# Query and key projections of layer 1 by seven block products in place of eight

## The chip, the cores and the metric

The kernel runs on one core of a Trainium2 chip. The metric is the device time of one execution in microseconds (us). The kernel before takes 2162.17 us as the median of 3 runs (2159.51 to 2166.93).

## The reference, cut to what matters

128 graphs of 64 nodes with 256 features pass through four layers, each as `x = x + layer(relu(layernorm(x)))`, all in float32. Layer 0 mixes over the graph and runs four small LSTMs over windows of the nodes. Layer 1 is a graph convolution, then attention with 4 heads of 64, then a two-layer MLP:

```python
h = relu(layernorm(einsum('mn,bnf->bmf', L_norm, x) @ Wc + bc))
x1 = h + x
q, k, v = x1 @ Wq, x1 @ Wk, x1 @ Wv            # split into 4 heads
o = softmax(mask(q @ k.T / sqrt(64))) @ v      # per graph and head
x2 = layernorm(x1 + o @ Wo + bo)
out = layernorm(x2 + gelu(x2 @ W1 + b1) @ W2 + b2)
```

Layer 2 is a second attention, layer 3 a spectral step with the eigenvectors of a Laplacian. The change is in `q` and `k`: the product of a 256x256 weight with the transposed tokens.

## The kernel before, in words

Tokens are handled in tiles of 128 (two graphs); there are 64 tiles. Layer 0 takes them in 8 groups of 8 tiles, the later layers ("the rest", layers 1 to 3) in 16 groups of 4 tiles, which is 512 tokens. Layer 0 writes its result to memory ("put"), and a rest group fetches its 4 tiles from there. The eigenvectors are worked out on VectorE beside layer 0.

The order of the work is not the order in which it is written. Every operation is recorded (so all instructions have one line, L344) and a planner, `Plan.schedule`, lists them for each engine in turn. It knows a cost for each operation, the buffers of each pool and what each operation depends on, keeps several rest groups in flight (8 of them), ranks by group and by the length of the path still ahead, and adds 0.4 us of distance between a producer on another engine and a TensorE operation of the rest (`slack`). Each engine then executes its list in order: an instruction that waits holds up everything behind it on its engine. So any edit to the recorded operations can move others. Small 64x64 products are kept together in bursts of 32 or 16 (`plan.burst()`), and TensorE changes between bursts and other work as seldom as the planner can arrange.

The pools that matter: `bank`, the 8 PSUM banks of 128x512; `big`, buffers of 128x1024 in SBUF, to which the spaces called `arena`, `sums`, `mids` and parts of `Whh` are added once layer 0 is done with them; `stat`, small ones for the statistics of layer norms. Weights of layers 1 to 3 are loaded by SyncE's queue (SP) into the space of LSTM weights (`Wih`, `Whh`) as these become free near the end of layer 0; `Carver` deals that space out. That is why a layer 1 weight shows in the profile as `Wih` or `Whh`, and a `big` buffer often as `arena`, `sums` or `mids`.

In layer 1 (`layer1`), once `x1` is done, `to_fm` transposes it to `x1T` (2 chunks of 128 features by 512 tokens) by 8 transposes and 2 copies out of PSUM. `proj_fm` then makes half of `qT` or `kT` by two products of 128x512 that accumulate in one bank; `evac` copies the bank to SBUF, on VectorE if its last argument is even and on ScalarE if it is odd. So q and k take 8 products of 128x512 and 4 copies of 128x512, two of them on each engine. After the softmax `pT` (transposed attention) and `oT` (the attention's output) are each copied out by one copy on VectorE and one on ScalarE.

Layer 0 has the 7-product scheme already: `lstm_fast` splits weights and inputs into 2x2 blocks, `pieces` makes four sums of the input blocks, and `fastw` holds the sums of weight blocks. There, each of the seven products is a pair of matmuls (input and hidden part).

Of the kernel before, what the change touches and what calls it, by code (L numbers as in the profile page):

```python
# [8 lines left out]
ALU = mybir.AluOpType  # L9
# [878 lines left out]
P = 128  # L888
# [4 lines left out]
HT = 4  # L893
# [39 lines left out]
def gnn_kernel(ctx: ExitStack, tc: tile.TileContext, a, out):  # L933
# [4 lines left out]
    def C(shape, name):  # L938
        return pool.tile(list(shape), F32, name=name)
# [3 lines left out]
    wih = [C([P, 2 * (3 if p == 0 else 4) * D], f"Wih{p}") for p in range(4)]  # L943
    whh = [None] + [C([P, 8 * D], f"Whh{p}") for p in range(1, 4)]
# [36 lines left out]
    plan = Plan(tc, {"PE": nc.tensor, "V": nc.vector, "ACT": nc.scalar, "G": nc.gpsimd, "SP": nc.sync}, pools, late, reserve, window, EIG, REST + NT // HT - 6, slack)  # L981
    PE, V, ACT, G, SP = (plan.proxy(e) for e in ("PE", "V", "ACT", "G", "SP"))

    def bank(name):
        return plan.value("bank")

    def load(t, src):
        SP.dma_start(t, src)
        return t

    def chunks(src):
        return src.rearrange("(c p) f -> p c f", p=P)
# [25 lines left out]
    Wg = [load(C([P, 2, D], f"Wg{i}"), chunks(a[f"Wg{i}"])) for i in range(2)]  # L1018
# [59 lines left out]
    for p in (1, 2):  # L1078
        fastw[p] = []
        for i, w in enumerate((Wih[p], Whh[p])):  # L1080
            a11, a12, a21, a22 = (w.rearrange("p k (q m n) -> p k q m n", q=4, m=2)[:, k, :, m, :] for m in range(2) for k in range(2))
            s1, s2, s4 = (space.tile([P, 4, P]) for j in range(3))
            s3 = a21 if i else space.tile([P, 4, P])
# [21 lines left out]
    room = Carver(arena)  # L1105
# [53 lines left out]
    flat = lambda t: t.rearrange("p t f -> p (t f)")  # L1159
# [17 lines left out]
    def tm(n=HT, f=D):  # L1177

        return plan.value("big")[:, :n * f].rearrange("p (t f) -> p t f", f=f)

    def fm():

        return plan.value("big")[:, :2 * HT * P].rearrange("p (c n) -> p c n", c=2)
# [4 lines left out]
    def transposes(srcs):  # L1188

        pt = bank("tr")  # L1190
        for i, s in enumerate(srcs):
            PE.transpose(pt[:, i * P:(i + 1) * P], s, ident)
        return pt
# [51 lines left out]
    def pieces(B, eng):  # L1245

        n = B(0, 0).shape
        w = 1
        for k in n[1:]:
            w *= k  # L1250
        t = plan.value("big")[:, :4 * w].rearrange("p (i n) -> p i n", i=4)
        t = [t[:, i] for i in range(4)]
        if len(n) == 3:
            t = [v.rearrange("p (w t) -> p w t", t=n[2]) for v in t]
        eng.tensor_tensor(t[0], B(0, 1), B(0, 0), op=ALU.subtract)
        eng.tensor_tensor(t[1], B(1, 1), t[0], op=ALU.subtract)
        eng.tensor_tensor(t[2], B(1, 1), B(0, 1), op=ALU.subtract)
        eng.tensor_tensor(t[3], B(1, 0), t[1], op=ALU.subtract)
        return {1: B(0, 0), 2: B(1, 0), 3: B(1, 1), 4: t[3], 5: t[0], 6: t[1], 7: t[2]}
# [128 lines left out]


    plan.group = WEIGHTS  # L1390
    room = Carver(wih[1], whh[1], wih[2], whh[2], wih[0])
    wtile = lambda src: load(room.tile([P, src.shape[0] // P, src.shape[1]]), chunks(src))
    btile = lambda src, n=D: load(room.tile([P, n]), src.to_broadcast([P, n]))
    ctile = lambda shape, src: load(room.tile(shape), src)
    Wc, Wq, Wk, Wv, W1, W2, Wo = (wtile(a[n]) for n in ("Wc", "Wq", "Wk", "Wv", "W1", "W2", "Wo"))
# [2 lines left out]

    g2c, be2c = (ctile([P, 2], a[n].rearrange("o (c p) -> p (o c)", p=P)) for n in ("g2", "be2"))
    G.tensor_tensor(b2, b2, be2, op=ALU.add)  # L1400
    W2a = wtile(a["L2_W"])

    wa = room.tile([P, 2, D])
    WT, a12 = fm(), wtile(a["L2_a"])
# [25 lines left out]
    def evac(dst, src, i):  # L1430
        if i % 2:
            ACT.copy(dst, src)
        else:
            V.tensor_copy(dst, src)
# [8 lines left out]
    def proj_fm(w, src, m):  # L1443
        ps = bank("fm")
        for c in range(2):
            PE.matmul(ps, w[:, c, tok(m)], src[:, c, :], start=c == 0, stop=c == 1)
        return ps

    def proj_tm(lhs, w, nk, t0):

        ps = bank("tm")
        for t in range(2):
            for c in range(nk):
                PE.matmul(ps[:, t * D:(t + 1) * D], lhs(c, t0 + t), w[:, c, :], start=c == 0, stop=c == nk - 1)
        return ps
# [29 lines left out]
    def layer1(x):  # L1485
        h = relu_norm(x)
        lx = mix_fm(h, lambda t: lapb)
        x1 = tm()
        for t0 in (0, 2):
            ps = proj_tm(lambda c, t: lx[:, c, tok(t)], Wc, 2, t0)  # L1490
            V.tensor_add(x1[:, t0:t0 + 2, :], ps.rearrange("p (t f) -> p t f", t=2), vec(bc, 2))
        norm(x1)
        for t0 in (0, 2):
            xp, hp = x1[:, t0:t0 + 2, :], h[:, t0:t0 + 2, :]
            V.tensor_mul(xp, xp, vec(g1, 2))
            G.tensor_add(xp, xp, vec(be1, 2))
            V.scalar_tensor_tensor(xp, xp, 0.0, hp, op0=ALU.max, op1=ALU.add)
        x1T = to_fm(x1)
        qT, kT, v = fm(), fm(), tm()
        for m in range(2):  # L1500
            evac(qT[:, m, :], proj_fm(Wq, x1T, m), 0)
            evac(kT[:, m, :], proj_fm(Wk, x1T, m), 1)
        for t0 in (0, 2):
            evac(pair(v, t0), proj_tm(lambda c, t: x1T[:, c, tok(t)], Wv, 2, t0), 1)
        for t0 in (0, 2):
            G.tensor_add(x1[:, t0:t0 + 2, :], x1[:, t0:t0 + 2, :], vec(bo, 2))


        ps = [bank("qk") for m in range(2)]
        with plan.burst():  # L1510
            for b, m, r in [(b, m, r) for b in range(2 * HT) for m in range(2) for r in range(2)]:
                PE.matmul(ps[m][half(r ^ m), bat(b)], qT[half(r), m, bat(b)], kT[half(r), m, bat(b)], start=True, stop=True)
        s = tm(4 * HT, N)
        for m in range(2):
            sm = s[:, m * 2 * HT:(m + 1) * 2 * HT, :]
            V.scalar_tensor_tensor(sm, ps[m].rearrange("p (b k) -> p b k", k=N), 0.125, vec(mask1, 2 * HT), op0=ALU.mult, op1=ALU.add)
            stat = plan.value("stat")
            softmax_shift(sm, stat[:, :2 * HT])
            ACT.activation(sm, sm, AF.Exp)
            ssum = stat[:, 2 * HT:4 * HT]  # L1520
            V.reduce_sum(ssum, sm, axis=AX.X)
            V.reciprocal(ssum, ssum)
            G.tensor_mul(sm, sm, ssum.unsqueeze(2).to_broadcast([P, 2 * HT, N]))

        pT = fm()
        for m in range(2):
            evac(pT[:, m, :], transposes([flat(s[:, (m * HT + t) * 2:(m * HT + t) * 2 + 2, :]) for t in range(HT)]), m)
        oT = fm()

        po = [bank("o") for i in range(2)]  # L1530
        with plan.burst():
            for m, t, i, r in [(m, t, i, r) for m in range(2) for t in range(HT) for i in range(2) for r in range(2)]:
                PE.matmul(po[i][half(r), bat(m * HT + t)], v[half(i), t, bat(2 * m + r)], pT[half(i), m, bat(2 * t + (r ^ m))], start=True, stop=True)
        for i in range(2):
            evac(oT.rearrange("p c (t b n) -> p c t b n", t=HT, b=2)[:, :, :, i, :], po[i].rearrange("p (c t n) -> p c t n", c=2, t=HT), i)
        x2 = tm()
        for t0 in (0, 2):
            ps = proj_tm(lambda c, t: oT[:, c, tok(t)], Wo, 2, t0)
            V.tensor_add(x2[:, t0:t0 + 2, :], ps.rearrange("p (t f) -> p t f", t=2), x1[:, t0:t0 + 2, :])
        norm(x2)  # L1540
        x2T = fm()
        for c in range(2):
            ACT.activation(x2T[:, c, :], transposes([x2[:, t, tok(c)] for t in range(HT)]), AF.Identity, scale=g2c[:, c:c + 1], bias=be2c[:, c:c + 1])
        V.tensor_mul(x2, x2, vec(g2))
        for t0 in (0, 2):
            G.tensor_add(x2[:, t0:t0 + 2, :], x2[:, t0:t0 + 2, :], vec(b2, 2))
        mT = [fm() for i in range(2)]
        for m in range(4):
            ACT.activation(mT[m // 2][:, m % 2, :], proj_fm(W1, x2T, m), AF.Gelu, bias=b1[:, m:m + 1])
        for t0 in (0, 2):  # L1550
            ps = proj_tm(lambda c, t: mT[c // 2][:, c % 2, tok(t)], W2, 4, t0)
            V.tensor_add(pair(x2, t0), ps, pair(x2, t0))
        for t0 in (0, 2):
            G.tensor_add(x[:, t0:t0 + 2, :], x[:, t0:t0 + 2, :], vec(be3, 2))
        norm(x2)
        for t0 in (0, 2):
            V.tensor_mul(x2[:, t0:t0 + 2, :], x2[:, t0:t0 + 2, :], vec(g3, 2))
            V.tensor_add(x[:, t0:t0 + 2, :], x[:, t0:t0 + 2, :], x2[:, t0:t0 + 2, :])
# [115 lines left out]
```

## Time and profile before

| | |
|---|---|
| median of 3 runs | 2162.17 us |
| the profiled execution's own time | 2164.86 us |
| its span, first to last instruction | 2163.1 us |
| TensorE (PE) busy | 2117.6 us, 98% |
| VectorE (DVE) busy | 1795.0 us, 83% |
| ScalarE (ACT) busy | 1066.5 us, 49% |
| GpSimd (POOL) busy | 650.6 us, 30% |
| granted TensorE clock, mean | 0.993 |

The page gives busy time by engine, then the span in 40 slices with busy tenths, then the chain that ended last, then groups of instructions as `out<-in`, with count, busy time, mean duration of one, and the idle time of the engine just before them. A float32 matmul leaves two MATMUL records (16580 records in all). A record's end is modelled, so durations of successive matmuls overlap; the pace is read from the starts. Layer 0 ends at about 1367 us of the span; the rest groups, which begin to be mixed in at 1222 us, fill what follows.

### The profile page before, as it was taken

What the parts mean: (1) busy time and instruction counts of PE and PEld (TensorE: products, weight loads), DVE (VectorE), ACT (ScalarE), POOL (GpSimd) and SP (SyncE); (2) the same over time, 40 slices, a digit from 0 to 9 for tenths busy, and PEclk for the clock granted to TensorE, in tenths of its full rate; (3) what the DMA queues carried; (4) which work ended last, traced back from release to release, by engine and by line L of the source; (5) the groups of instructions that cost most, each with busy time, mean ns of one, the idle gap of its engine ahead of it and who ended that gap; (6) DMA issues with size and microseconds to landing.
All of it is one profiled execution on the core that took longest, in us unless ns stands there. A gap on an engine that the chain in (4) does not pass through costs nothing. (4 is left out here: it accounts for less than half of the span.)

```text
span 2163.1 us, 45587 instructions
## 1 busy us (share of the span) xinstructions
PE 2117.6 (98%) x16580; PEld 1632.8 (75%) x16580; DVE 1795.0 (83%) x7402; ACT 1066.5 (49%) x2321; POOL 650.6 (30%) x968
## 2 busy tenths in 40 slices
PE   9999999999999999999999999999999999999997
PEld 6688688688678688678778788767677777676776
DVE  5788888888899999889989887777887778875796
ACT  3354354354344344345345343555556656545673
POOL 7211221210200110110110101675456555644353
PEclk9999999999999999999999999999999999999999
DMA  5000100100100100100000111200010000000001
GB/s 205 1 3 22 41 3 21 40 1 21 40 1 20 40 1 20 40 1 20 26 1 21 52 44 44 89 1 21 1 41 21 22 21 21 11 21 2 1 2 60
DMA packets 44865, 57.66 MB, mean 27 GB/s; under 512 B 8928, under 2 KB 38496, under 8 KB 44640
## 3 DMA queue, kind: packets, MB, share of 16 engines
q1 hardware_dynamic: 43536, 53.71, 7.5%
q8 instruction: 130, 2.13, 0.4%
q10 hardware_dynamic: 1104, 1.05, 0.2%
q14 instruction: 95, 0.78, 0.1%
HBM read 37.53 MB, written 16.78 MB: 25 GB/s over the span
## 5 line engine op out<-in xcount | busy, mean ns | idle before, releaser
L344 PE MATMUL bank<-big,Wih 128*128 128x256 f32 (+3 forms) x2400 | 751.8, 436 | 14.4 <-DVE arena L344 6.7
L344 PEld LDWEIGHTS bank<-big,Wih 128*128 128x128 f32 x2400 | 440.3, 191 | 194.0 <-issue 112.1
L344 ACT ACTIVATE mids<-bank,bl 128x256 f32<-128x256 f32 (+3 forms) x528 | 274.6, 526 | 387.5 <-PE bank L344 385.3
L344 PE MATMUL bank<-big,Whh 128*128 128x256 f32 (+2 forms) x1624 | 431.5, 367 | 3.7 <-DVE big L344 3.7
L344 DVE TENSOR_TENSOR arena<-arena 64x21 f32<-64x21 f32 (+5 forms) x2251 | 372.1, 195 | 29.8 <-POOL arena L344 1.3
L344 PEld LDWEIGHTS bank<-big,Whh 128*128 128x128 f32 x1624 | 294.1, 190 | 42.8 <-issue 9.9
L344 PE MATMUL bank<-big,sums 128*128 128x168 f32 (+2 forms) x1664 | 267.5, 310 | 0.3
L344 POOL TENSOR_SCALAR stat<-stat 128x4 f32<-128x4 f32 (+1 forms) x228 | 71.1, 313 | 561.8 <-DVE stat L344 547.9
L344 PEld LDWEIGHTS bank<-big,sums 128*128 128x128 f32 (+1 forms) x1664 | 223.6, 179 | 17.2 <-issue 4.5
L344 ACT COPY mids<-bank 128x168 f32<-128x168 f32 (+2 forms) x378 | 124.8, 349 | 147.7 <-PE bank L344 142.9
L344 DVE TENSOR_TENSOR big<-mids 128x512 f32<-128x512 f32 (+2 forms) x256 | 141.8, 563 | 36.1 <-ACT mids L344 32.9
L344 ACT ACTIVATE mids<-mids,bl 128x336 f32<-128x336 f32 (+3 forms) x192 | 102.0, 539 | 77.6 <-DVE mids L344 73.6
L344 DVE SCALAR_TENSOR_TENSOR arena<-arena 64x1 f32<-64x1 f32 (+15 forms) x565 | 122.3, 239 | 6.2 <-POOL arena L344 2.5
L344 POOL TENSOR_TENSOR stat<-stat,mhalf 128x4 f32<-128x4 f32 (+1 forms) x114 | 121.9, 1070 | 6.4
L344 ACT ACTIVATE mids<-big 128x256 f32<-128x256 f32 (+2 forms) x176 | 89.4, 510 | 67.6 <-DVE big L344 48.0
L344 DVE TENSOR_TENSOR mids<-bank,mids 128x168 f32<-128x168 f32 (+1 forms) x294 | 103.1, 356 | 8.4 <-PE bank L344 4.7
L344 DVE TENSOR_SCALAR arena<-arena 64x1 f32<-64x1 f32 (+8 forms) x533 | 103.1, 200 | 8.4 <-POOL arena L344 0.4
L344 DVE TENSOR_TENSOR big<-big,mids 128x256 f32<-128x256 f32 (+2 forms) x192 | 93.7, 488 | 11.0 <-ACT mids L344 10.0
L344 POOL TENSOR_TENSOR big<-big 128x168 f32<-128x168 f32 (+1 forms) x24 | 15.8, 671 | 262.0 <-DVE arena L344 135.8
L344 POOL TENSOR_TENSOR arena<-arena 64x1 f32<-64x1 f32 x66 | 44.8, 678 | 152.6 <-ACT arena L344 106.3
L344 DVE BATCH_NORM_STATS2 stat<-big 128x6 f32<-128x256 f32 x228 | 83.2, 406 | 4.9 <-DMA big<-put 4.0
L344 ACT COPY big<-bank 128x512 f32<-128x512 f32 x90 | 49.5, 586 | 58.0 <-PE bank L344 55.9
(366 smaller groups left out, 3663.0 us busy)
## 6 DMA issues: line engine op xcount, KB each, us to landing
big<-in_x_dram SPq DMA_DIRECT2D x30, 512.0 KB, 5.3
put<-big SPq DMA_DIRECT2D x16, 512.0 KB, 2.8
arena<-put SPq DMA_DIRECT2D x8, 512.0 KB, 6.8
out_dram<-arena SPq DMA_DIRECT2D x16, 256.0 KB, 2.2
big<-put SPq DMA_DIRECT2D x7, 512.0 KB, 4.4
out_dram<-big SPq DMA_DIRECT2D x14, 256.0 KB, 2.4
Wih<-in_WihT_dram SPq DMA_DIRECT2D x3, 1024.0 KB, 12.1
Whh<-in_WhhT_dram SPq DMA_DIRECT2D x3, 1024.0 KB, 13.8
```

What stands on the lines that cost most here:

```text
L344: getattr(self.engines[op.eng], name)(*map(real, args), **{k: real(a) for k, a in kw.items()})
```

## The change

Four edits:

1. When weights are loaded, three new 128x128 tiles for each of Wq and Wk are made on GpSimd, by four operations per weight; the fourth result overwrites a block of the weight itself. The tiles come out of the same space as the other weights (768 columns), so some later tiles get other places, and the space of `Wg` is added at the end of the list.
2. Per rest group, `pieces` makes four 128x256 sums of blocks of `x1T` on GpSimd, in one more `big` buffer.
3. `proj_fast` replaces two `proj_fm` and two `evac` for q, and the same for k: seven products of 128x256 where there were four of 128x512. Two banks are held; results are read out of PSUM while the bank goes on accumulating: four copies of 128x256 on ScalarE and three additions of 128x256 on VectorE.
4. The copies of `pT` and `oT` that were on VectorE are on ScalarE.

```diff
+    room = Carver(wih[1], whh[1], wih[2], whh[2], wih[0], *(w.rearrange('p c f -> p (c f)') for w in Wg))
+    fastp = {}
+    for nm, w in (("Wq", Wq), ("Wk", Wk)):
+        a11, a12, a21, a22 = (w[:, k, m * P:(m + 1) * P] for m in range(2) for k in range(2))
+        s1, s2, s4 = (room.tile([P, P]) for j in range(3))
+        s3 = a21
+        G.tensor_tensor(s1, a21, a22, op=ALU.add)
+        G.tensor_tensor(s2, s1, a11, op=ALU.subtract)
+        G.tensor_tensor(s3, a11, a21, op=ALU.subtract)
+        G.tensor_tensor(s4, a12, s2, op=ALU.subtract)
+        fastp[nm] = {1: a11, 2: a12, 3: s4, 4: a22, 5: s1, 6: s2, 7: s3}
+    def proj_fast(L, R, dst):
+        w = HT * P // 2
+        a, b = bank("fast"), bank("fast")
+        a, c, b = a[:, :w], b[:, :w], b[:, w:2 * w]
+        lo, hi = ([dst[:, m, n * w:(n + 1) * w] for n in range(2)] for m in range(2))
+        def prod(ps, i, start=False):
+            PE.matmul(ps, L[i], R[i], start=start, stop=True, skip_group_check=True)
+        with plan.burst(3 * (0.001672 * w + 0.006)):
+            prod(a, 1, True)
+            prod(c, 2, True)
+            prod(b, 5, True)
+        ACT.copy(lo[0], a)
+        ACT.copy(hi[1], b)
+        V.tensor_tensor(lo[0], c, lo[0], op=ALU.add)
+        prod(a, 6)
+        ACT.copy(lo[1], a)
+        prod(b, 3)
+        V.tensor_tensor(lo[1], b, lo[1], op=ALU.add)
+        prod(a, 7)
+        V.tensor_tensor(hi[1], a, hi[1], op=ALU.add)
+        prod(a, 4)
+        ACT.copy(hi[0], a)
...
-        for m in range(2):
-            evac(qT[:, m, :], proj_fm(Wq, x1T, m), 0)
-            evac(kT[:, m, :], proj_fm(Wk, x1T, m), 1)
+        R = pieces(lambda c, n: x1T[:, c, n * HT * P // 2:(n + 1) * HT * P // 2], G)
+        proj_fast(fastp["Wq"], R, qT)
+        proj_fast(fastp["Wk"], R, kT)
...
-            evac(pT[:, m, :], transposes([flat(s[:, (m * HT + t) * 2:(m * HT + t) * 2 + 2, :]) for t in range(HT)]), m)
+            evac(pT[:, m, :], transposes([flat(s[:, (m * HT + t) * 2:(m * HT + t) * 2 + 2, :]) for t in range(HT)]), 1)
...
-            evac(oT.rearrange("p c (t b n) -> p c t b n", t=HT, b=2)[:, :, :, i, :], po[i].rearrange("p (c t n) -> p c t n", c=2, t=HT), i)
+            evac(oT.rearrange("p c (t b n) -> p c t b n", t=HT, b=2)[:, :, :, i, :], po[i].rearrange("p (c t n) -> p c t n", c=2, t=HT), 1)
```

More of the change, by code (lines that the diff above doesn't have):

```diff
@@ L1390, in gnn_kernel @@
     plan.group = WEIGHTS
-    room = Carver(wih[1], whh[1], wih[2], whh[2], wih[0])
+    room = Carver(wih[1], whh[1], wih[2], whh[2], wih[0], *(w.rearrange('p c f -> p (c f)') for w in Wg))
     wtile = lambda src: load(room.tile([P, src.shape[0] // P, src.shape[1]]), chunks(src))
```

## The prediction

> **What bounds the kernel now.** I read the page from the top: busy shares, slices, chain.
>
> ```profile
> PE 2117.6 (98%) x16580; PEld 1632.8 (75%) x16580; DVE 1795.0 (83%) x7402; ACT 1066.5 (49%) x2321; POOL 650.6 (30%) x968
> ...
> PE   9999999999999999999999999999999999999997
> ...
> PE 33%; DVE 4%; ACT 1%; POOL 1%; DMA 1%; issue 1%; SPq 0%; DVEq 0%; ACTq 0%; POOLq 0%
> ```
>
> PE fills every slice but the last and leads the chain. Busy PE is not PE at its peak, so I took the pace from the timeline, in a dense stretch:
>
> ```profile
> 1959.59 1.88 PE L344 MATMUL bank<-sums,Wih 128*128 128x512 f32 x4
> 1961.31 1.02 PE L344 MATMUL bank<-mids,Whh 128*128 128x512 f32 x2
> 1962.17 1.03 PE L344 MATMUL bank<-Whh,arena 128*128 128x256 f32 x4
> 1963.03 1.03 PE L344 MATMUL bank<-Wih,big 128*128 128x256 f32 x4
> ```
>
> Two records are one product. From start to start, 4 records of 512 columns take 1.72 us and 4 of 256 take 0.86 us: 0.86 and 0.43 us a product (medians over all 0.858 and 0.432). Half the columns cost half the time, so seven half-width products really are cheaper. Then busy time by stretch (columns: stretch, length, PE, PEld, DVE, ACT, POOL): start of the rest, middle, tail.
>
> ```profile
> 1375.00:1425.00 50.00, 45.63 (x656) 34.94 (x656) 40.82 (x120) 34.05 (x63) 44.72 (x63) 0.93 0.15 58
> 1425.00:2075.00 650.00, 644.41 (x6590) 470.43 (x6589) 505.34 (x1395) 377.19 (x662) 343.57 (x455) 1.00 0.05 15
> 2075.00:2163.10 88.10, 75.29 (x1195) 61.57 (x1193) 69.46 (x215) 44.18 (x82) 37.53 (x57) 0.97 0.11 38
> ```
>
> In the middle PE is 99% busy, DVE 78%, ACT 58%, POOL 53%: PE alone bounds it. At the start POOL is at 89%. Subtracting each operation's pace from the distance to the next start, I get PE's lost time: 9.9 us from 1375 to 1450, 20.3 from there to 2075 (clock dips and changes to and from 64x64 bursts included), 14.3 in the tail. Only 44.5 of some 790 us are not streaming: removed streaming should show. The chain in order of time says what the start waits for:
>
> ```profile
> 1369.42 5.82 DMA big<-put
> ...
> 1377.35 1.05 POOL stat L344
> ...
> 1382.57 20.42 PE bank L344 x326
> ```
>
> A fetch, statistics, GpSimd's power and a ScalarE pass lie ahead of PE's work.
>
> **What the skill says.** The Trainium skill, "TensorE: Matmul & The Clock Gate", Back-to-back issue gap, gives 262 cycles for 256 columns and 518 for 512 per pass, nearly proportional; the 0.432 and 0.858 us above agree. "ScalarE: Activation LUTs", What ACT_TABLE_LOAD costs, gives about 1283 ns and a drain of about 1380 ns; here the load takes 1283 ns, and in the timeline one ends at 1543.76 with the next pass at 1543.77, so I count no drain. "SBUF — State Buffer", Who interferes with whom, says that a DVE instruction with two SBUF inputs contends with a GpSimd instruction that reads SBUF: the new GpSimd sums read SBUF, while the new DVE additions have one input in PSUM. The trace has a case: next to a POOL operation at 1700.12 a DVE pass took 0.82 us where its twins took 0.41.
>
> **The change part by part.** Durations, from the groups by shape (mean ns of one after the busy time; the copies of 128x512 have 586 on ACT and 682 on DVE):
>
> ```profile
> L344 ACT COPY mids<-bank 128x256 f32<-128x256 f32 x160 | 53.9, 376 | 67.2 <-PE bank L344 67.1
> ...
> L344 DVE TENSOR_TENSOR mids<-bank,mids 128x256 f32<-128x256 f32 x100 | 41.1, 416 | 4.2 <-PE bank L344 2.6 <-issue 0.4 <-ACT mids L344 0.2
> ...
> L344 POOL TENSOR_TENSOR big<-big,big 128x256 f32<-128x256 f32 x24 | 16.9, 730 | 2.6 <-DVE big L344 1.6 <-DVE arena L344 0.7
> ...
> L344 ACT ACT_TABLE_LOAD x39 | 50.0, 1283 | 19.2 <-PE bank L344 15.0 <-DMA adjT<-in_adjT_dram 3.6
> ```
>
> *PE stream.* Per group 8 x 0.858 = 6.86 us go, 14 x 0.432 = 6.05 come. Over 16 groups 109.8 - 96.8 = 13.0 us less.
>
> *Burst changes.* In the built order of the changed kernel PE changes between 64x64 bursts and other work 126 times in the rest, before 116. A product ahead of a burst lasts 0.952 instead of 0.858 us, a burst ahead of a product 1.043 instead of 0.981: 0.16 us a pair, five pairs, +0.8.
>
> *DVE.* Per group four copies of 512 leave (2.73 us), six additions come (2.50): -0.2 us. Nothing, behind PE.
>
> *ACT.* Per group eight copies of 256 and the two moved ones come (3.01 + 1.17), the two of kT leave (1.17): +3.0 us. Also, the new order has 55 table loads for 39: 16 x 1.283 = 20.5 us, or 1.3 a group. ACT goes from 58% to about 67% of the middle; hidden by PE as long as no product waits for a copy behind a load. Six of the 55 loads have a new copy among their next three instructions: at most 6 x 1.28 = 7.7 us.
>
> *POOL, per group.* Four sums, 4 x 0.73 = 2.9 us: 53% to about 59% in the middle, hidden. If they hold DVE up as in the case above, DVE has 22% to spare.
>
> *POOL, once.* Eight sums of 128x128: by the line through 579 ns (168 columns) and 730 ns (256) 0.51 us each, 4.1 in all. They are queued in the stretch 1264 to 1307, where POOL is nearly idle; behind them stand an addition and statistics of the first rest group, whose consumer on PE is at 1364. Nothing; without that cover, 4.1 us.
>
> *Loads.* The same DMAs go through SP. The product that needs the attention vectors of layer 2 moves on PE from 1362 to about 1304, before the last LSTM steps, and the vectors' load is queued seven places earlier (landing 2.4 us after issue, before). I expect it in time; late by one landing it is +2.4. The stall of 2.8 us that PE has at 1314.8, behind a DVE operation that waits for a bias load, stays: its last LSTM reader and its place at the end of SP's queue are the same. Net 0, between -2.8 and +2.4.
>
> *New waits on PE.* Bank `a` is read between products 1, 6, 7 and 4, `b` between 5 and 3. Behind a waiting product stands all of PE. In the new order the stream from the start of the first three products to product 6 is 2.1 us or more in all 32 projections, mostly 2.6 to 3.5. Product 1 is done at 0.43; a copy of 0.38 and hand-overs of a few tenths fit, and POOL needs 0.73 a sum. Layer 0's `lstm_fast` is the nearest row: it reads its banks in the same way, and PE loses under 0.1 us from 600 to 725. Both ends: 0, and 0.5 us for each of 32 projections, 16. I take +1.5.
>
> *Start of the rest.* GpSimd's list from layer 0's end: the new one has the four sums and both bias additions of group one (2.9 + 2.7 = 5.6 us) ahead of the statistics of group two. By durations, POOL finishes the additions ahead of group two's transposes 30.4 us after its start, about 1367; PE reaches them 33.1 us after 1364.8. Group two's sums end at 39.9 against PE at 38.3. Counting the passes between, PE waits 1 to 4 us. The first groups' own PE saving (0.8 each) goes into waiting for fetches too. Ends 0 and 8 (nearly three groups' sums); I take +3.
>
> *Tail.* The last 110 scheduled operations on PE and on DVE are the same ones in the same order: 0.
>
> Sum: -13.0 + 0.8 + 1.5 + 3 = -7.7 us. Against the profiled execution: span 2163.1 to 2155.4, own time (1.8 more) 2157.1. The median shown is 2.7 below that time: 2154.5.
>
> **The rivals.** *PE waits inside the projections.* Each becomes a hand-over from PE to ACT or DVE and back; a copy may stand behind an Exp, a Gelu (0.7 us) or a table load. For it: 16 more loads, and 28.5 us that weight loads already wait for ACT over 39 times, the longest 3.5 us:
>
> ```profile
> PEld bank L344 <- ACT mids L344: 28.5, 39, 3.5
> ```
>
> Against it: the distances in the order, and layer 0. Without this term the sum is -9.2; waits of 0.29 us a projection use that up, more make it slower. At 0.65 it is 20.8 us: -9.2 + 20.8 = +11.6, 2174.
>
> *GpSimd becomes the bound at the start.* For it: 89% there already, and 14.7 us of its work per group ahead of the attention products against some 16 of PE. Against it: PE has four groups' other work in between. With 8 us instead of 3: -2.7, 2159.5. That would be no measurable gain.
>
> *The redrawn order is better.* The order is a list from estimates; the start lost 9.9 us and the middle 20.3. If PE regains half of the start and sees no new waits: -13.0 + 0.8 - 5 = -17, at most; I take -15, 2147. For it: the new list gives PE groups three to five before attention of group one. Against it: POOL.
>
> That the change doesn't do what it says can be excluded: the new order has 32 products of 128x256 fewer than twice the 128 of 512 that leave.
>
> **How the numbers follow.** No-change and change can be told apart beyond about 0.3%, 6.5 us: below 2155.7 or above 2168.7. Chances: likeliest 0.55, waits 0.15, GpSimd 0.2, better order 0.1. The likeliest runs from 2150 (waits and start at 0) to 2160 (at 4 and 5.5); 0.44 of its 0.55 I put below 2155.7. Faster: 0.44 + 0.1 = 0.54. Same: 0.11 + 0.2 = 0.31. Slower: 0.15. The range 2147 to 2166 holds the likeliest, GpSimd and part of the third.
>
> **What would show it.** PE's lost time in the middle near 22 us; PE's records 16772 (192 more); table loads 1283 ns and 55; POOL busy about 50 us more, ACT about 68 more, DVE about 4 less; the first rest groups' statistics later on POOL by some 6 us. I am wrong if waits of PE for ACT or POOL grow by over 10 us in the middle, or the start's lost time passes 18.

## Result, and the profile after

The changed kernel takes 2151.74 us as the median of 4 runs (2150.66 to 2154.98), the kernel before 2162.57 us in the same 4 rounds (2159.51 to 2166.93). The ratio is 0.9947, with a 95% interval of 0.9934 to 0.9959: 10.8 us faster, where 7.7 were forecast. The forecast median of 2154.5 us is missed by 2.8 us. The two profiled executions differ by more, 2164.86 - 2151.09 = 13.8 us (spans 2163.1 and 2149.3), because that of before lies 2.3 us above its median and that of after 0.7 below.

The page of the changed kernel: busy shares, slices of PE, chain by engine.

```profile
PE 2102.0 (98%) x16772; PEld 1665.0 (77%) x16772; DVE 1796.7 (84%) x7434; ACT 1124.1 (52%) x2465; POOL 708.4 (33%) x1040
...
PE   9999999999999999999999999999999999999998
...
PE 79%; DVE 11%; POOL 3%; issue 3%; ACT 2%; DMA 2%; SPq 0%; DVEq 0%; ACTq 0%; POOLq 0%
```

PE is still the bound, with 15.6 us less of busy time. ACT and POOL have 58 us more each, DVE 2 more. The pace of PE, from its timeline (start, time, matmuls, records):

```profile
1704.56 0.59 PE L344 MATMUL bank<-Wih,sums 128*128 128x256 f32 x2
1704.99 1.88 PE L344 MATMUL bank<-big,Whh 128*128 128x512 f32 x4
1706.71 0.59 PE L344 MATMUL bank<-big,same 128*128 128x256 f32 x2
```

0.43 us from start to start for 256 columns, 1.72 for two products of 512: the pace is that of before. Busy time by stretch (stretch, length, PE, PEld, DVE, ACT, POOL, granted clock, share and GB/s of DMA), for the start of the rest, its middle and the tail:

```profile
1375.00:1425.00 50.00, 47.04 (x577) 39.72 (x576) 44.62 (x125) 33.98 (x70) 47.91 (x62) 1.00 0.05 18
1425.00:2075.00 650.00, 639.58 (x6868) 500.87 (x6867) 506.85 (x1429) 439.36 (x802) 393.86 (x522) 1.00 0.05 15
2075.00:2149.30 74.30, 62.72 (x1031) 53.77 (x1029) 58.32 (x184) 34.48 (x66) 29.96 (x45) 0.98 0.13 44
```

In the middle PE's share falls from 99.1% to 98.4%: 4.8 us of 650 have opened up. POOL rises to 61% there and ACT to 68%; at the start POOL is at 96%. The chain in order of time across the start (start, time, what):

```profile
1364.56 5.67 DMA arena<-put
...
1372.94 2.40 POOL stat L344 x4
...
1378.10 3.75 POOL arena L344 x3
...
1393.24 6.97 PE bank L344 x35
```

The fetch starts 4.9 us earlier than before. Behind it GpSimd holds more of the chain than it did: besides statistics, 3.75 us of additions on `arena`, so that the chain comes back to PE at 1393.24 us, where it was at 1382.57. PE has other work meanwhile: its waits from 1360 to 1425 us add up to 2.8 us, before 4.4. The groups by shape (count, busy time, mean ns of one, idle time before them):

```profile
L344 ACT COPY mids<-bank 128x256 f32<-128x256 f32 x188 | 64.1, 377 | 73.0 <-PE bank L344 72.5
...
L344 DVE TENSOR_TENSOR mids<-bank,mids 128x256 f32<-128x256 f32 x120 | 49.2, 416 | 10.9 <-PE bank L344 5.7 <-ACT mids L344 3.7 <-issue 0.4
...
L344 POOL TENSOR_TENSOR big<-big,big 128x256 f32<-128x256 f32 x30 | 21.4, 733 | 2.6 <-DVE big L344 1.6 <-DVE arena L344 0.7
...
L344 ACT ACT_TABLE_LOAD x55 | 70.6, 1283 | 35.9 <-PE bank L344 18.0 <-DVE mids L344 9.0 <-DVE sums L344 4.4
```

The durations are those that the prediction used, and there are 55 table loads. Where the time went, by PE's lost time (the distance between starts less each operation's pace; worked out from both traces as for the prediction, but with the middle ending at the last 110 scheduled operations on PE):

| | before, us | after, us | difference | predicted |
|---|---|---|---|---|
| stream without any loss | 2059.1 | 2046.1 | -13.0 | -13.0 |
| lost in layer 0 (to 1075 us) | 38.5 | 35.3 | -3.2 | 0 |
| lost at the end of layer 0 (to about 1364 us) | 13.2 | 10.8 | -2.4 | 0 |
| lost in the first 50 us of the rest | 9.7 | 5.3 | -4.4 | +3 |
| lost in the middle | 23.4 | 34.7 | +11.3 | +2.3 |
| lost in the tail | 14.2 | 11.8 | -2.4 | 0 |

The differences add up to -14.1 us, the spans differ by -13.8. So the sum came near with one term too small and several too large. Part of the gains lies in PE's clock. The trace of before has six stretches of 3.4 to 8.1 us in which it is granted at half speed (the last outlasts the span), which costs up to 15.0 us; the trace of after has two, which cost 5.1. Those at 232 and 894 us more than account for layer 0, those at 1382 and 1413 us for 3.4 us at the start.

The runs show the clock too. Over 100 runs of the kernel before, the mean granted clock lies between 0.993 and 0.998, and a run is some 1.3 us shorter for each 0.001 more. Those 100 runs have a mean of 0.995, the four of the changed kernel one of 0.997, so by estimate 2 to 3 us of the 10.8 come with the clock. The gain doesn't rest on it: `after_slack45` below gains 12.1 us at a mean of 0.995.

### The profile page after: what moved, and what is told of

The parts are those of the page before. It is cut to its first block, busy times and chain, and to the rows that moved or that the text cites. A ratio compares the mean times of both kernels' runs of the same rounds, so it can differ in the third digit from the quotient of the medians.

```text
span 2149.3 us, 46200 instructions
## 1 busy us (share of the span) xinstructions
PE 2102.0 (98%) x16772; PEld 1665.0 (77%) x16772; DVE 1796.7 (84%) x7434; ACT 1124.1 (52%) x2465; POOL 708.4 (33%) x1040
## 4 chain that ended last, share of the span: by engine, by line
PE 79%; DVE 11%; POOL 3%; issue 3%; ACT 2%; DMA 2%; SPq 0%; DVEq 0%; ACTq 0%; POOLq 0%
PE bank L344 79%; DVE stat L344 3%; DVE arena L344 3%; DVE big L344 3%; POOL stat L344 2%; DVE mids L344 1%; DVE sums L344 1%; DMA big<-in_x_dram 1%; ACT big L344 1%; ACT mids L344 1%; POOL arena L344 0%; ACT arena L344 0%; POOL big L344 0%; DVE Whh L344 0%; SPq L344 0%
## 5 line engine op out<-in xcount | busy, mean ns | idle before, releaser
L344 PE MATMUL bank<-big,Wih 128*128 128x256 f32 (+3 forms) x2408 | 731.7, 426 | 14.7 <-DVE arena L344 6.9
L344 PE MATMUL bank<-big,Whh 128*128 128x256 f32 (+2 forms) x1692 | 448.0, 366 | 1.5 <-DVE big L344 1.4
L344 PEld LDWEIGHTS bank<-big,Whh 128*128 128x128 f32 x1692 | 306.8, 190 | 40.6 <-issue 8.6
L344 ACT COPY mids<-bank 128x168 f32<-128x168 f32 (+2 forms) x427 | 146.2, 364 | 151.9 <-PE bank L344 146.0
L344 DVE TENSOR_TENSOR mids<-bank,mids 128x168 f32<-128x168 f32 (+2 forms) x322 | 116.1, 368 | 25.1 <-PE bank L344 17.6
L344 ACT ACTIVATE mids<-big 128x256 f32<-128x256 f32 (+2 forms) x176 | 89.4, 510 | 62.7 <-DVE big L344 46.3
L344 POOL TENSOR_TENSOR big<-big 128x168 f32<-128x168 f32 (+1 forms) x30 | 21.4, 726 | 272.5 <-DVE arena L344 105.7
L344 PE MATMUL bank<-Wih,big 128*128 128x256 f32 x384 | 94.1, 383 | 3.1 <-DVE big L344 0.9
L344 POOL TENSOR_TENSOR arena<-arena 64x1 f32<-64x1 f32 (+1 forms) x70 | 46.8, 669 | 145.9 <-ACT arena L344 105.8
```

Of the source, the lines that this page charges most:

```text
L344: getattr(self.engines[op.eng], name)(*map(real, args), **{k: real(a) for k, a in kw.items()})
```

## Experiments

Each label is compared with runs of the kernel before on the same chip; "gain" is the difference of the two medians. The changed kernel's gain is 10.8 us. Most kernels go through the planner again, and their whole order is redrawn; three keep the order of the changed kernel: `twice`, `evac_v_same_order` and `sums_v_same_order`, each with an instruction issued once more or on another engine.

**Is it the stream?** In the kernel before, an eighth of q's and k's stream is left out.

```diff
+        def proj_less(w, src, m):
...
+            n = 256 if m == 0 else 512
+            PE.matmul(ps[:, :n], w[:, 1, tok(m)], src[:, 1, :n], start=False, stop=True, skip_group_check=True)
...
-            evac(qT[:, m, :], proj_fm(Wq, x1T, m), 0)
-            evac(kT[:, m, :], proj_fm(Wk, x1T, m), 1)
+            evac(qT[:, m, :], proj_less(Wq, x1T, m), 0)
+            evac(kT[:, m, :], proj_less(Wk, x1T, m), 1)
```

> The kernel before, with only TensorE work taken away: in each half of q and k that has m = 0 the second product covers 256 of the 512 columns (the other half of the result lacks that term, so q and k are incomplete). Per group 2 x (0.858 - 0.432) = 0.85 us of stream, 13.6 us over 16 groups, with no new operation on ScalarE, VectorE or GpSimd. Theory (TensorE's stream bounds the rest, saved stream shows in full): 2162.5 - 13.6 = about 2149, give or take 2. Rival (the gain of the change came from the redrawn order and the clock, the stream saved is mostly given back): 2157 to 2162.

2150.99 us against 2163.4, ratio 0.9945 (0.9932 to 0.9957): a gain of 12.4 us for the 13.6 of stream, within what the theory said. This kernel is planned anew, so the agreement is good only to the size of a redrawn order (below). In the changed kernel, the other way round, one product of each projection is issued twice:

```diff
             prod(c, 2, True)
+            prod(c, 2, True)
```

> The changed kernel in its own order, with product 2 of each projection issued twice (the second overwrites the first, so the result is the same): 32 x 0.432 = 13.8 us of TensorE stream come back and nothing else changes. Theory (TensorE's stream bounds the rest also in the changed kernel): 2151.7 + 13.8 = about 2165, give or take 2. Rival (in the changed kernel VectorE, ScalarE and GpSimd set the pace, and the lost time of the middle, 34.7 us, takes the extra products in): 2152 to 2159.

2164.31 against 2164.1, ratio 1.0003 (0.9995 to 1.0011): 32 products of 0.432 us, 13.8 us of stream, take away 11.0 us of the gain, in an unchanged order; again the theory's value is met, and not the rival's. Of what is added to or taken from PE's stream, four fifths or more appear in the time.

**Do the reads between the products cost?** All seven products first, then the seven reads:

```diff
-        with plan.burst(3 * (0.001672 * w + 0.006)):
...
+        prod(a, 6)
+        prod(b, 3)
+        prod(a, 7)
+        prod(a, 4)
         ACT.copy(lo[0], a)
...
```

> The changed kernel with all seven products of a projection issued without a read between them, and the seven reads after the last (q and k are then wrong, the amount of work is the same). Theory (in the middle of the rest the products that come after a read of their bank lose 5.7 us in all): 2146 to 2149. Rival (the reads between the products cost nothing, the added lost time comes from the rest of the order): 2151 to 2153, as the changed kernel.

2167.46 against 2163.4, ratio 1.0018 (1.001 to 1.0027): 4.1 us slower than before, outside both expectations. PE's lost time in the middle is 43.8 us in its trace, with waits for several engines, none large. The planner redrew the order, and a redrawn order can cost more than the effect that was looked for. Three more runs size that.

Where the time is lost can still be read: the planner's list gives the operation of each of PE's records. With one pace for each shape, from 1425 to 2075 us, the products of q and k lose 2.7 us in this kernel and 6.1 in the changed one, and all other operations 40.8 and 28.5. So at these products the reads cost some 3 us, and this kernel is slow in operations that it shares with the changed one.

**What does a redrawn order cost by itself?** `room` is the kernel before with the changed kernel's placement of weights and nothing else; `before_slack45` and `after_slack45` plan the two kernels with another distance.

```diff
-    room = Carver(wih[1], whh[1], wih[2], whh[2], wih[0])
+    room = Carver(wih[1], whh[1], wih[2], whh[2], wih[0], *(w.rearrange('p c f -> p (c f)') for w in Wg))
...
+    for j in range(6):
+        room.tile([P, P])
```

> The kernel before with only the placement of edit 1: the six tiles are dealt out but not filled, and the space of Wg is added to the list. Theory: only what happens at the end of layer 0 moves, the stall of 2.8 us on TensorE behind the bias load goes or stays: 2159 to 2163. Rival (placement and the new order are what made the change faster): 2156 or below.

```diff
-            return 0.4 if op.group >= REST and op.group != EIG else 0.12
+            return 0.45 if op.group >= REST and op.group != EIG else 0.12
```

> The kernel before with the same number changed. Theory (redrawing): off 2163.4 by 2 to 9 us, either way; with the run before this one it tells how much of a difference of two kernels planned anew is chance. Rival: 2162 to 2165.

> The changed kernel with one number of the planner changed, the distance ahead of TensorE's operations in the rest, 0.45 us for 0.40: the same operations in a redrawn order. Theory (a redrawn order alone moves the time by several us, as the kernel with only the placement did, 5.8): off 2151.7 by 2 to 9 us, either way. Rival (the order is not worth more than 1.5 us): 2150 to 2153.

`room`: 2169.22, ratio 1.0026 (1.0015 to 1.0038), 5.8 us slower than before, so both its expectations missed. `before_slack45`: 2166.88, 1.0015 (1.0007 to 1.0022), 3.9 us slower, as its theory said. `after_slack45`: 2150.89, 0.9945 (0.9932 to 0.9957), a gain of 12.1; here the rival stands, the order moved this kernel by 1.3 us. So the same work in another order moves by up to some 6 us, and a smaller difference between two orders proves nothing. The changed kernel keeps its gain over two orders. In four orders without the seven-product scheme (before, `before_slack45`, `room` and `evac_alone` below) PE loses 23.4, 28.8, 29.1 and 26.5 us in the middle, 27 on average; in two orders of the changed kernel 34.7 and 28.8. The scheme costs some 5 us there on these averages, and 11 in the pair that was compared. The working by operation, as for `no_partial` (its totals are within 2.5 us of these), says where:

| lost in the middle, us | products of q, k and the first MLP weight | all other operations |
|---|---|---|
| before | 4.2 | 21.0 |
| `before_slack45` | 6.0 | 25.2 |
| `room` | 4.7 | 26.8 |
| `evac_alone` | 3.7 | 22.5 |
| `pe_less` | 3.3 | 25.6 |
| changed kernel | 7.8 | 26.8 |
| `after_slack45` | 6.0 | 23.3 |

The products lose 4.4 us on average without the scheme and 6.9 with it. The other operations, which the change doesn't touch, lose 24.2 and 25.0 on average, but 21.0 and 26.8 in the pair that was compared: more than half of that pair's difference lies in them.

**What is edit 4 worth?** Undone in the changed kernel (`evac_back`, the diff), and made alone in the kernel before (`evac_alone`, the reverse of it), both replanned:

```diff
-            evac(pT[:, m, :], transposes([flat(s[:, (m * HT + t) * 2:(m * HT + t) * 2 + 2, :]) for t in range(HT)]), 1)
+            evac(pT[:, m, :], transposes([flat(s[:, (m * HT + t) * 2:(m * HT + t) * 2 + 2, :]) for t in range(HT)]), m)
...
-            evac(oT.rearrange("p c (t b n) -> p c t b n", t=HT, b=2)[:, :, :, i, :], po[i].rearrange("p (c t n) -> p c t n", c=2, t=HT), 1)
+            evac(oT.rearrange("p c (t b n) -> p c t b n", t=HT, b=2)[:, :, :, i, :], po[i].rearrange("p (c t n) -> p c t n", c=2, t=HT), i)
```

> The changed kernel with edit 4 undone: one copy of pT and one of oT go back to VectorE. Theory (VectorE and ScalarE both have room, edit 4 is worth nothing): within 2 us of the changed kernel, 2150 to 2154. Rival (the gain needs VectorE relieved): slower than the changed kernel by 4 us or more, 2156 or above.

> The kernel before with edit 4 alone, planned anew. Theory (no effect of its own, only a redrawn order): anywhere in 2157 to 2171. Rival (VectorE relieved is a gain): 2153 to 2157.

`evac_back`: 2160.22 against 2163.4, ratio 0.9987 (0.9979 to 0.9995), so 7.6 of the 10.8 us go, as the rival said. `evac_alone`: 2161.69 against 2163.03, ratio 1.0002 (0.9993 to 1.001): nothing, as the theory said. Both are replanned, so I repeated the first within the changed kernel's own order, by issuing one copy of `pT` and one of `oT` per group on VectorE at the same places. The operation is planned as ScalarE's, and only its issue differs (one call of `evac` for `pT` and one for `oT` pass 9):

```diff
+        if i == 9:
+            ACT.copy(dst, src)
+            op = plan.ops[-1]
+            op.calls[0] = ("tensor_copy",) + op.calls[0][1:]
+            op.to = "V"
...
-                    getattr(self.engines[op.eng], name)(*map(real, args), **{k: real(a) for k, a in kw.items()})
+                    getattr(self.engines[getattr(op, 'to', op.eng)], name)(*map(real, args), **{k: real(a) for k, a in kw.items()})
```

> The changed kernel's own order and buffers, planned with the copies on ScalarE, but one copy of pT and one of oT in each group are issued on VectorE instead, at the places where they stood. So edit 4 is half undone without redrawing the order. Theory (edit 4 by itself is worth about nothing, and the 8.5 us that its undoing cost came from the redrawn order): 2149.5 to 2154.5. Rival (copies on VectorE hold up what TensorE waits for): 2157 or above, near the 2160 of the kernel with edit 4 undone and planned anew.

2156.91 against 2163.03, ratio 0.998 (0.997 to 0.9989), apart from the 0.9934 to 0.9959 of the changed kernel: 4.7 us of the gain go, so the theory fails, and the rival comes near: it said 2157 or above. Some 22 us of copies (32 of 0.68) moved from ScalarE to VectorE lengthen the kernel by 4.7, while VectorE is idle in about a fifth of the middle. (The mean clock of these runs is 0.996, so by the estimate above up to 1 us of it may be the clock.) What PE waits for in the middle (total, times, longest) tells a part. The changed kernel:

```profile
PE bank L344 <- DVE arena L344: 2.6, 4, 1.1
PE bank L344 <- DVE big L344: 2.1, 3, 1.7
```

The same order with those copies on VectorE:

```profile
PE bank L344 <- DVE big L344: 4.0, 6, 1.7
PE bank L344 <- DVE arena L344: 3.6, 4, 1.9
```

The waits of PE for VectorE grow by 2.9 us in these two lines.

**Which engine should make the sums?** On VectorE, once replanned (`sums_dve`) and once in the changed kernel's own order (`sums_v_same_order`, with the same use of `op.to`):

```diff
-        R = pieces(lambda c, n: x1T[:, c, n * HT * P // 2:(n + 1) * HT * P // 2], G)
+        R = pieces(lambda c, n: x1T[:, c, n * HT * P // 2:(n + 1) * HT * P // 2], V)
```

```diff
         R = pieces(lambda c, n: x1T[:, c, n * HT * P // 2:(n + 1) * HT * P // 2], G)
+        for op in plan.ops[-4:]:
+            op.to = "V"
```

> The changed kernel with the four sums per group made on VectorE instead of GpSimd, planned anew: GpSimd 64 x 0.73 = 47 us less, VectorE 64 x 0.41 = 26 us more (1.7 a group, from 78% to about 81% of the middle). Theory (VectorE, not GpSimd, is what TensorE waits for in the projections; copies on VectorE cost 5 to 8 us): 2155 or above. Rival (GpSimd's sums and their collisions with VectorE make the added lost time): 2150 or below. A redrawn order alone moves a kernel by about 4 us, so between these it tells nothing.

> The changed kernel in its own order and buffers, with the four sums of each group issued on VectorE at the places where they stood for GpSimd. Planned anew this cost 28 us. Theory (work added to VectorE, 1.7 us a group, is what costs, order aside): 2160 to 2185. Rival (the 28 us came from the redrawn order): 2150 to 2156.

`sums_dve`: 2179.9 against 2163.46, ratio 1.0074 (1.0061 to 1.0087), 16.4 us slower than before. `sums_v_same_order`: 2169.76 against 2164.1, ratio 1.0028 (1.0018 to 1.0038), 5.7 slower. Both theories stand. In the same order, 26 us of work on VectorE (64 sums of about 0.41) take away more than the gain, 16.5 us (up to 3 of them by the clock, whose mean is 0.995 here). Its PE waits in the middle:

```profile
PE bank L344 <- DVE arena L344: 6.8, 8, 1.9
PE bank L344 <- DVE big L344: 3.8, 5, 1.6
PE bank L344 <- DVE sums L344: 2.5, 3, 1.2
```

VectorE is busy for 522.81 us of the 650 in this run, 80%, and PE's lost time there is 46.3 us in place of 34.7. By operation, products 3 and 4 of the projections, which VectorE's additions release, lose 9.5 us here and 3.7 in the changed kernel; so about half of the 11.6 us lost more is the queue ahead of these additions, and the rest is spread over other operations. A mean of 80% thus does not mean that an engine has a fifth to spare. The sums take 47 us on GpSimd (64 of 0.73) and are cheaper there than 26 on VectorE.

**Would more of the same help?** The first MLP weight by seven products too, with GpSimd's sums, ScalarE's copies and a Gelu of its own:

```diff
-    for nm, w in (("Wq", Wq), ("Wk", Wk)):
+    for nm, w in (("Wq", Wq), ("Wk", Wk), ("W1a", W1[:, :, :D]), ("W1b", W1[:, :, D:])):
...
+            proj_fast(fastp[nm], R, mT[i])
+            for m in range(2):
+                ACT.activation(mT[i][:, m, :], mT[i][:, m, :], AF.Gelu, bias=b1[:, 2 * i + m:2 * i + m + 1])
```

> The changed kernel with the first MLP product (W1, 256x512) made in the same way, as two projections by seven products, Gelu then from SBUF: another 16 x 2 x (6.86 - 6.05) / 2 = 13.0 us of TensorE stream less, per group again 4 sums on GpSimd (2.9 us), 8 copies of 256 on ScalarE (3.0) and 6 additions on VectorE (2.5). Theory (the stream saved shows, less about 10 us of new lost time and a few us of longer chains in the tail): 2145 to 2152. Rival (VectorE at some 83% and GpSimd at 66% give it all back): 2154 or above.

2163.18 against 2163.46, ratio 0.9995 (0.9987 to 1.0003). Another 13.0 us of stream less, and the whole gain is gone, as the rival said. The middle by engine:

```profile
1425.00:2075.00 650.00, 626.47 (x6920) 533.60 (x6919) 537.44 (x1506) 453.52 (x895) 439.58 (x576) 1.00 0.05 15
```

PE is down to 96% while VectorE is at 83%, ScalarE at 70% and GpSimd at 68%; PE's lost time there is 52.9 us. No single engine has become the bound; PE waits for one or another of three. The loss is at the scheme's own products this time: those of q, k and the first MLP weight lose 21.1 us (7.8 in the changed kernel), the others 30.9 (26.8). None of the runs is clearly faster than the changed kernel.

## Why the prediction was right, and where it was not

**The main term was right.** The stream fell by the 13.0 us that the count of products gave, and `twice`, in an unchanged order, shows that four fifths of PE's stream pass into the time; `pe_less` agrees.

**Burst changes and new waits on PE, +2.3 together, were too small:** +11.3 in the two traces, some +5 over several orders; the lost time of the middle was expected near 22 us and was 34.7. In size the term was not far off: the products lose 2.5 us more with the scheme, on average over the orders, and the rest of the +11.3 lies in other operations, mostly with the order. Where the waits would be it had wrong, because it followed the wrong hand-over. It compared product 6 with ScalarE's copy of the bank, and that does hold: products 6 lose 0.8 us in all over the middle. The losses are at product 4, the last one, which waits until VectorE has added bank `a` to the output: 3.5 of the 6.1 us that the products of q and k lose there. One wait of 1.65 us makes up half of it, and in `after_slack45` product 4 loses 0.5 us in all, so this too depends on the order. That wait in the timeline:

```profile
1480.20 3.09 DVE L344 TENSOR_TENSOR mids<-mids,stat 128x512 f32<-128x512 f32 x2
...
1481.25 1.49 POOL L344 TENSOR_TENSOR arena<-arena,stat 128x512 f32<-128x512 f32 x1
...
1483.81 1.26 DVE L344 TENSOR_REDUCE stat<-mids 128x8 f32<-128x512 f32 x2
...
1485.00 0.41 DVE L344 TENSOR_TENSOR big<-bank,big 128x256 f32<-128x256 f32 x1
...
1485.55 0.67 PE L344 MATMUL bank<-sums,Wih 128*128 128x256 f32 x2 [1.65 <-DVE big L344]
```

The addition takes 0.41 us, but it stands behind five passes of VectorE, of which the first two, beside work of GpSimd, take 1.5 us each; such passes take 0.68 where GpSimd does nothing. The prediction bounded a wait by 0.5 us for each projection, and the mean stays below that; this one has 1.65.

**"Nothing, behind PE" for DVE, and its 22% to spare, was the step that failed.** It priced VectorE's work by its mean share (and VectorE is busy for 2 us more, not 4 less). `sums_v_same_order` and `evac_v_same_order` give the price: 16.5 us for 26 and 4.7 for 22. By the same step edit 4 would have been worth nothing; within this order it is worth 4.7 us. The forecast did not suffer, since the edit stays in. `evac_alone` fits the step: without the new additions the relief of VectorE brought nothing, but that kernel was planned anew, so this is not shown at a fixed order. That PE's new waits for VectorE are the reason is what the waits above suggest; in `sums_v_same_order` products 3 and 4 account for 5.8 of the 16.5 us, but in `evac_v_same_order` the waits cover 2.9 of the 4.7 us and the products of the scheme lose only 0.9 us more, so mostly other operations wait there.

The slowing of VectorE beside GpSimd is where the Trainium skill, "SBUF — State Buffer", Who interferes with whom, was used: a VectorE instruction with two SBUF inputs contends with a GpSimd instruction that reads SBUF. The trace agrees. Over the middle, VectorE's passes of 128x512 that take a statistic from SBUF beside their data have a mean of 1.03 us over 28 (0.84 over 30 before, both worked out from the groups by shape), while those with an input in PSUM stay at 0.68. In sum it grew little: all TENSOR_TENSOR passes of this shape with both inputs in SBUF have a mean of 0.82 us over 108, before 0.80 over 111. So as an amount the prediction could dismiss it. What it missed is again the place: two slowed passes ahead of one addition hold up a product, as in the lines above.

**ACT: hidden, right, and nearly in its amount.** +58 us busy for about +68. PE's waits for ScalarE in the middle amount to 2.0 us in the changed kernel, 1.3 before. The weight loads' wait over the whole run, which the first rival rested on, has hardly moved:

```profile
PEld bank L344 <- ACT mids L344: 30.0, 45, 3.5
```

So the first rival's mechanism exists, but through VectorE and at a smaller price. The order has the 16 more table loads that were forecast, and little came of them.

**POOL per group: hidden, right** (+58 us for about +50; the sums take 0.73 us each where nothing collides and up to 1.2 where it does, and GpSimd's passes of this shape have a mean of 0.79 in the rest).

**Start of the rest, +3, did not come, and the second rival with it.** GpSimd does get tighter there (96% busy), but PE doesn't wait for it more than before. The prediction added GpSimd's sums and bias additions to the time before group two's statistics. GpSimd in the changed kernel around the end of layer 0:

```profile
1357.49 0.99 POOL L344 MEMSET Wih<- 128x512 f32 x2 [2.46 <-PE bank L344]
1360.63 1.43 POOL L344 TENSOR_TENSOR big<-big 128x256 f32<-128x256 f32 x2 [2.15 <-ACT big L344]
...
1366.85 0.23 POOL L344 TENSOR_SCALAR stat<-stat 128x4 f32<-128x4 f32 x1 [0.95 <-DVE stat L344]
1367.17 1.04 POOL L344 TENSOR_TENSOR stat<-stat,mhalf 128x4 f32<-128x4 f32 x1
```

And in the kernel before:

```profile
1361.33 0.99 POOL L344 MEMSET Wih<- 128x512 f32 x2 [2.46 <-PE bank L344]
1365.69 2.52 POOL L344 TENSOR_TENSOR big<-big,Wih 128x512 f32<-128x512 f32 x2 [3.37 <-PE bank L344]
1370.65 0.23 POOL L344 TENSOR_SCALAR stat<-stat 128x4 f32<-128x4 f32 x1 [2.44 <-DVE stat L344]
1370.97 1.04 POOL L344 TENSOR_TENSOR stat<-stat,mhalf 128x4 f32<-128x4 f32 x1
```

From the MEMSET, GpSimd's last work for layer 0, to the first power of the statistics is 9.7 us after and 9.6 before. The sums fit where GpSimd used to wait (3.37 us for PE and 2.44 for VectorE), and it still waits 0.95 us for VectorE's part of the statistics. The prediction expected these 6 us later; they are not later at all. It laid GpSimd's instructions end to end, counted the two bias additions as new although they (2.52 us) stand ahead of these statistics before as well, and left out that the list already had idle places. Of the 4.4 us that PE loses less at the start, 3.4 are the half-speed stretches of the trace before. One of them follows a wait of 2.6 us for the ScalarE pass that ends the prediction's chain, and neither is in the trace after.

**Loads: 0, and it was -2.4.** The stall of PE behind a bias load of layer 2 was said to stay. VectorE in the changed kernel waits for the load here:

```profile
1312.71 0.23 DVE L344 TENSOR_SCALAR Whh<-Whh 128x128 f32<-128x128 f32 x1 [1.51 <-DMA Whh<-in_L_b_dram]
```

And in the kernel before:

```profile
1316.93 0.23 DVE L344 TENSOR_SCALAR Whh<-Whh 128x128 f32<-128x128 f32 x1 [3.99 <-DMA Whh<-in_L_b_dram]
```

The prediction's 2.8 us of PE stalled are gone: VectorE's wait is 1.51 us, and PE, still busy with layer 0's products, does not feel it. The load is issued 1.8 us earlier and lands 4.6 us after its issue, where it took 7.0; why it lands sooner was not looked into. The value lay inside the range given for the step (-2.8 to +2.4). That the product with the attention vectors would be in time was right: it does not wait.

**Tail, 0:** the same 110 operations in the same order, and -2.4 in the traces. The clock doesn't explain it: the half-speed stretch that ends the trace before holds only 2.1 us of PE's work, that in the tail of the trace after 3.4. The cause stays open. The third rival, a better order, isn't needed: what looks like it at the start is the clock and the idle GpSimd.

So that the sum of -7.7 came near the -10.8 measured is in part luck: the terms missed in both directions.

**Left open:** what makes one order lose more than another outside the projections (from 21.0 us before to 39.2 in `no_partial`), and which of the other operations wait when VectorE has more to do.

## What to carry to other kernels

On a kernel that one engine bounds at 98%, count that engine's stream first, and then look for the last hand-over in each new chain: which engine releases the last product, and what stands ahead of that release in its list. A mean share of 78% on the releasing engine is no slack; test a suspected engine by issuing the same instruction on another engine in the same order, because a replanned order of the same work moves by as much as the effect (here up to 6 us of 2160). A scheme that trades stream for work on the other engines paid once here and not twice: the second use gave back all.

## What the runs showed of the hardware

PE's granted clock falls to half for stretches of 3.4 to 10.2 us. In these traces they tend to follow a pause of PE. All 14 traces have a pause of 2.2 us at about 230 us, and in 12 of them such a stretch starts within 3 us of its end; after the pause of 2.7 us at about 893 us it is 8 of 14, after one of 1.4 us at 400 us none. The changed kernel's trace has neither that at 232 nor that at 894. So the same pause is followed by a slow stretch in one run and not in another; what decides it was not tried. The stretches make a difference of 10 us between the two traces shown, so a trace is not a median.

A VectorE pass of 128x512 with two inputs in SBUF can take 1.5 us in place of 0.68 beside GpSimd. In the changed kernel's trace GpSimd's passes of 128x256 take 0.73 us on average where no such VectorE pass runs beside them and 0.84, up to 1.2, where one does: both sides lose.
